# A row LSTM on normalised images: the first row of one half moved into the statistics, late rows moved from GpSimd to ScalarE

## The chip, the cores and the metric

The kernel runs on one core of a Trainium2 chip. The metric is the device time of one execution in microseconds. Five engines work side by side, each through its own list of instructions in order: TensorE (PE in the profile, with PEld for its weight loads), VectorE (DVE), ScalarE (ACT), GpSimd (POOL) and SyncE (SP), which here issues every transfer. An engine waits only where an instruction needs what another engine or a transfer has not delivered yet.

## The reference

The input x has 8 images of 96 channels, 128 rows and 128 columns. It is normalised in 32 groups of 3 channels (mean and variance over channels, rows and columns of a group), run through a row LSTM, and added to the result.

```python
its = conv(X, W_is * mask)                 # 1x3, masked, 96 -> 384 channels
def step(carry, row_in):                   # over the 128 rows
    h, c = carry
    ss = conv1d(h, W_ss)                   # 3 taps along the columns
    g5 = (ss + row_in).reshape(B, 3, 4, Oc, Wd)
    f, i, o = sigmoid(g5[:, :, 0]), sigmoid(g5[:, :, 1]), sigmoid(g5[:, :, 2])
    g = tanh(g5[:, :, 3])
    c_new = f * c + i * g
    h_new = o * tanh(c_new)
x = x + row_lstm(gn(x))
```

A row cannot start before the row above has its h, so the 128 rows are a chain. Nothing can be normalised before an image's statistics are known, so x is read twice: once for the statistics, once, in blocks of rows, for the recurrence.

## The kernel before

**Statistics.** An image is read as 128 partitions of 12288 numbers, in 6 chunks of 2048 columns (1 MB each; 48 chunks in all), into a ring of 6 buffers, so that chunk k of every image uses buffer k. VectorE runs `bn_stats` (L669) on 4 pieces of 512 columns per chunk and `bn_aggr` (L675) per image. Chunk 2 of the first seven images goes to ScalarE instead: `sums_of` (L198) has GpSimd write the negative of one column (`base`, L199), and ScalarE sums differences and squares (L200, L203). `merge` (L205) joins both shares on GpSimd, `Scale` (L225) makes scale and shift of a half's four images with small matmuls (L237) and 8-column operations. SyncE issues the next chunk into a buffer as soon as its reader is done; `chunks` (L641) puts other loads into that order, by the number of chunks issued.

**The recurrence.** The images are split into two halves of four. A half-step is one row of one half; half-step n is row n//2 of half n%2, so the two halves alternate, and half-step n needs h of n-2. Each half-step has 21 matmuls (in the trace two records each): own products of the input (P, Q, E: L376 from `xs`), and four products of h with the three-tap weights, written with sums and differences of even and odd columns (`vs`, `vf` by VectorE, `vd` by GpSimd, L476). ScalarE or VectorE copies the first partial result (`m`, L416/L418), VectorE adds and subtracts (L421, L425), ScalarE makes the gates (L428, L432), VectorE the cell and h (L436 to L453). The order is written out by hand in `PERIOD` and `PRODUCTS`, by short names, and no scheduler changes it on TensorE, ScalarE, VectorE and GpSimd.

**Rows in blocks of 4.** Channels 64 to 95 of the input are normalised into `hx` beside h (`normalise_shared`, L331, "shared"). Channels 0 to 63 stand twice in `xr`; `own_image` (L318) widens one image's four rows (normalise into `xw`, L297), and `combine` (L308) writes even+odd and two differences into `xs`. Both run on GpSimd during the block before: `work(n)` (L527) says which parts follow half-step n in `finish(n)` (L545), after its `vd` and residual; `FIRST` (L516) lists them for the first eight half-steps. `load_rows` loads `xr`, `load` loads x itself.

**The seam.** `events` (L628) places work of half 0 among the statistics, by image and piece: its merge and scales in image 4, its rows in images 4 to 6, and half-step 0 inside image 7 up to its gates. After the last aggregation come half 1's scales (on VectorE), its first row (`own_row`, L324, widened on ScalarE), the rest of half-step 0, and half-step 1. Rows 1 to 3 of half 1's first block, the late rows, are loaded then (L691, L692) and normalised by GpSimd in `late(1)` to `late(3)` after half-steps 0, 1 and 3, one image and row at a time.

Of the kernel before, what the change touches and what calls it, by code (L numbers as in the profile page):

```python
# [7 lines left out]
F32 = mybir.dt.float32  # L8
AF = mybir.ActivationFunctionType
ALU = mybir.AluOpType  # L10
# [5 lines left out]
def strided(ap, offset, dims):  # L16

    return bass.AP(ap.tensor, ap.offset + offset, [ap.ap[0], *[list(d) for d in dims]])
# [3 lines left out]
def kernel(  # L22
# [3 lines left out]
    w: bass.AP,  # L26


    out: bass.AP,
):  # L30

# [22 lines left out]
    nc = tc.nc  # L54
    B, C, H, W = x.shape
    P = 128
    NH = 2
    BH = B // NH
# [16 lines left out]

    O4 = 4 * C
    wl = const.tile([P, w.shape[1]], F32, name="wl")
    wm = const.tile([P, 3, O4], F32, name="wm")
    wx = const.tile([P, 2, O4], F32, name="wx")
    tap = [wl[:, bass.ts(i, O4)] for i in range(5)]  # L80
    bias, bias2 = wl[:, 5 * O4 : 5 * O4 + 3], wl[:, 5 * O4 + 3 : 5 * O4 + 6]
    gm = wl[:, 5 * O4 + 6 :].rearrange("p (i q) -> p i q", i=3)
    wt = [tap[1], wm[:, 0, :], wm[:, 1, :], tap[2]]
    wo = [wx[:, 0, :], wx[:, 1, :], tap[3]]

    def load_weights():
        nc.sync.dma_start(wl, w)

    def make_weights():

# [82 lines left out]
                skip_group_check=True,  # L173
            )

    def first_rows(s, hi):

        t = xt[s, 0].rearrange("c b r w -> c b (r w)")[:, :, 0 : hi * W]
        nc.scalar.activation(t[C:P], t[C2:C], AF.Identity)
        for p in range(2):  # L180
            nc.scalar.activation(  # L181
                xr[s][p * C2 : (p + 1) * C2, :, 0 : hi * W], t[0:C2], AF.Identity
            )

# [4 lines left out]

    SHARE = CH / QW
    su = const.tile([P, B, 2], F32, name="su")
    base = const.tile([P, B], F32, name="base")

    def sums_of(b, xc):  # L198
        nc.gpsimd.tensor_scalar(base[:, b : b + 1], xc[:, 0:1], -1.0, None, ALU.mult)  # L199
        nc.scalar.activation(  # L200
            xc, xc, AF.Identity, bias=base[:, b : b + 1], accum_out=su[:, b, 0:1]
        )
        nc.scalar.activation(xc, xc, AF.Square, accum_out=su[:, b, 1:2])  # L203

    def merge(s, n):  # L205

        p = nc.gpsimd
        at = slice(s * BH, s * BH + n)
        u, v, t = su[:, at, 0], su[:, at, 1], const.tile([P, n], F32, name=f"mt{s}")
        mean, var = st[s][:, 0:n, 0], st[s][:, 0:n, 1]  # L210
        p.tensor_scalar(su[:, at, :], su[:, at, :], 1.0 / CH, None, ALU.mult)
        p.tensor_mul(t, u, u)
        p.tensor_sub(v, v, t)
        p.tensor_sub(u, u, base[:, at])
        p.tensor_sub(u, u, mean)
        p.tensor_scalar(t, u, SHARE, None, ALU.mult)
        p.tensor_add(mean, mean, t)
        p.tensor_mul(u, u, u)
        p.tensor_scalar(u, u, SHARE * (1.0 - SHARE), None, ALU.mult)
        p.tensor_sub(v, v, var)  # L220
        p.tensor_scalar(v, v, SHARE, None, ALU.mult)
        p.tensor_add(var, var, v)
        p.tensor_add(var, var, u)
# [70 lines left out]
        else:  # L294
            engine.tensor_scalar(dst, src, scale, shift, ALU.mult, ALU.add)  # L295

    def widen(engine, xw, i, n, s, j, lo):  # L297

        norm(
            engine,  # L300
            strided(xw[:, i, :], 0, [(W + 1, n), (J + 1, 2), (1, J)]),
            xr[s][:, j, lo * W : (lo + n) * W].rearrange("p (r j t) -> p r t j", r=n, t=2),
            0,
            1,
            s * BH + j,
        )
# [14 lines left out]
        widen(nc.gpsimd, xw[0], 0, R, s, j, 0)  # L321
        combine(xw[0], R, to[:, :, 0, j, :], to[:, :, 1:3, j, :])

    def own_row(engine, xw, s, r):  # L324

        to = xs[s][0]
        for j in range(BH):
            widen(engine, xw, j, 1, s, j, r)
        combine(xw, BH, to[:, r, 0], to[:, r, 1:3].rearrange("p t b j -> p b t j"))

    def normalise_shared(engine, s, k, j, lo, hi):  # L331
# [21 lines left out]
    class HalfStep:  # L353
# [31 lines left out]
        def own(self, a, i):  # L385

            low = a == order["A"] or (a == order["C"] and self.s == 0)
            rhs = self.xs[:, i].rearrange("p b j -> p (b j)")
            self.mm(a, i % 2, wo[i], rhs, slice(0, C2) if low else slice(C2, P))
# [111 lines left out]
        )  # L501

    SHARED = ((0,), (1,), (2, 3), ())

    def own(s, *images):
        return [(own_image, s, 1, j) for j in images]

    def shared(s, k, *images, rows=(0, R)):  # L510
        return [(normalise_shared, nc.gpsimd, s, k, j, *rows) for j in images]

    def late(r):
        return shared(1, 0, *range(BH), rows=(r, r + 1)) + [(own_row, nc.gpsimd, xw[0], 1, r)]

    FIRST = [  # L516
        late(1) + own(0, 0),
        late(2) + shared(0, 1, 0),
        own(0, 1, 2),
        late(3) + [(load_rows, 1, 1)] + shared(0, 1, 1),  # L520
        own(0, 3) + [(load_rows, 0, 2)] + shared(0, 1, 2, 3) + own(1, 0),
        own(1, 1, 2) + shared(1, 1, 0, 1),
        own(1, 3) + [(load_rows, 1, 2)] + shared(1, 1, 2, 3),
        [(own_image, 0, 2, 0)],
    ]

    def work(n):  # L527
        if n < len(FIRST):
            return FIRST[n]
        row, s = divmod(n, NH)  # L530
        k, r = divmod(row, R)
        parts = []
        if r == R - 1 and k + 2 < NB:
            parts.append((own_image, s, k + 2, 0))
        elif r < R - 1 and k + 1 < NB:
            parts.append((own_image, s, k + 1, r + 1))
        if k + 1 < NB:
            parts += shared(s, k + 1, *SHARED[r])
        if r == R - 2 and k + 2 < NB:
            parts.append((load_rows, s, k + 2))  # L540
        if n == len(FIRST):
            parts.append((own_image, 1, 2, 0))
        return parts

    def finish(n):  # L545
# [66 lines left out]
    NS = QW // SN  # L612
    A = Scale(0)

    def shared_rows(engine, s, hi):
        for j in range(BH):
            normalise_shared(engine, s, 0, j, 0, hi)

    def begin():
        do(-NH, "S F D")  # L620
# [3 lines left out]
    def at(image, n):  # L624
        return image * NS + n


    events = {  # L628
        at(4, 0) + 2: lambda: (merge(0, BH), A.means()),
        at(4, 0) + 8: lambda: (A.squares(nc.scalar), A.to_sbuf(), first_rows(0, R)),  # L630
        at(4, 0) + 16: lambda: (A.scale(nc.gpsimd), shared_rows(nc.scalar, 0, R)),
        at(5, 12): lambda: (own_image(0, 0, 0), own_image(0, 0, 1)),
        at(6, 12): lambda: (own_image(0, 0, 2), own_image(0, 0, 3)),
        at(6, 18): lambda: first_rows(1, 1),
        at(7, 1): lambda: (merge(1, BH - 1), spin(10, stats[6])),
        at(7, 6): begin,
        at(7, 11): lambda: do(0, "loA hiA"),
        at(7, 13): lambda: do(0, "loB hiB EA 0A 3A taA siA"),
        at(7, 15): lambda: do(0, "loC hiC EB EC 0B 3B taB siB 0C 3C"),
    }  # L640
    chunks = {  # L641
        6: load_weights,
        7: make_weights,
        16: lambda: load(0, 0, copy=False),
        40: lambda: load(1, 0, 0, 1, copy=False),
    }
    stats = []
# [1 line left out]
    for b in range(B):  # L649
        bst = g_pool.tile([P, NS, 6], F32, tag="bst", name=f"bst{b}")  # L650
        xb = x[b].rearrange("c h w -> (c h w)").rearrange("(p q) -> p q", p=P)
        done = 0
        for k in range(QW // CH):
            xc = ring[n % len(ring)]
            pieces = 2 if n in (0, B * QW // CH - 1) else 1
            for piece in range(pieces):
                size = CH // pieces
                nc.sync.dma_start(  # L658
                    xc[:, bass.ts(piece, size)], xb[:, bass.ds(k * CH + piece * size, size)]
                )  # L660
            n += 1
            if n in chunks:
                chunks[n]()
            by_act = k == 2 and b + 1 < B
            if by_act:
                sums_of(b, xc)
            for j in range(CH // SN):
                if not by_act:
                    nc.vector.bn_stats(bst[:, done, :], xc[:, bass.ts(j, SN)])  # L669
                    done += 1  # L670
                m += 1
                if m in events:
                    events[m]()
        stats.append(bst[:, 0:done, :].rearrange("c n s -> c (n s)"))
        nc.vector.bn_aggr(st[b // BH][:, b % BH, :], stats[b])  # L675

    do(0, "taC siC")
    Bh = Scale(1)
    Bh.means()
    do(0, "fg")  # L680
    Bh.squares(nc.vector)
    spin(5, wt[0][:, 0:256])
    do(0, "gt")
    Bh.scale(nc.vector)

    shared_rows(nc.vector, 1, 1)
    do(1 - NH, "S F")
    own_row(nc.scalar, xw[1], 1, 0)
    do(1 - NH, "D")
    do(0, "ce th")  # L690
    load_rows(1, 0, 1, R)  # L691
    load(1, 0, 1, R)  # L692
    for s in range(NH):
        if s == 0:
            load_rows(0, 1)
        load(s, 1)


    do(1, "1A 2A 1B 2B 1C 2C PA PB QA QB P+A PC QC cpA loA hiA cpB loB hiB cpC loC hiC")
    do(1, "ou' F' S' D' re'")  # L700
    for n in range(1, last + 2):
        for names in PERIOD:
            do(n, PRODUCTS[n % 2] if names == "X" else names)
# [53 lines left out]
```

## Time and profile before

Seven runs: median 2087.94 us, 2087.39 to 2088.57.

| what | value |
|---|---|
| the profiled execution's own time | 2087.81 us |
| its span, first to last instruction | 2086.0 us |
| busy: TensorE, VectorE, GpSimd, ScalarE | 93%, 82%, 69%, 63% |
| last `bn_aggr` ends | 138.89 us |
| first matmul of half-step 1 starts | 146.37 us |
| TensorE busy from 160 to 220 us | 18.18, 18.00 and 16.47 of each 20 us |
| TensorE busy from 220 us on | 20.00 of 20 us |

TensorE is busy all the time from about 220 us to the end. Before that the span falls into the statistics, where the transfers run at 370 to 430 GB/s, and a stretch of some 80 us in which the recurrence has begun but TensorE still has gaps. In the lines of a timeline the columns are the start, the time, the engine, the line of the kernel, the operation, output<-input, the shapes, the count, and in brackets how long the engine had idled before and what ended that.

### The profile page before, as it was taken

The page shows a single profiled execution, that of the slowest core. Times are in us where ns is not written, and L with a number is a line of the kernel's source. Part 1 is how long each engine was busy: PE and PEld are TensorE (multiplying, and loading weights), DVE is VectorE, ACT ScalarE, POOL GpSimd, SP SyncE. Part 2 cuts the span into 40 slices and gives each one's busy share as a digit, 9 for nine tenths or more (in the row PEclk, how much of TensorE's full clock was granted, in tenths as well). Part 3 has the DMA queues.
Part 4 walks back from the last instruction along what each step waited for, and adds up shares of the span by engine and source line. Part 5 has one row for each costly group of instructions (what it writes and reads, how often), then busy time and mean ns, then how long its engine had stood idle before and what let it go on. Part 6 is the DMA issues. An engine that isn't in the chain of part 4 may idle for free.

```text
span 2086.0 us, 31236 instructions
## 1 busy us (share of the span) xinstructions
PE 1949.4 (93%) x10810; PEld 1586.1 (76%) x10810; DVE 1703.5 (82%) x3522; ACT 1321.2 (63%) x2352; POOL 1445.8 (69%) x1636
## 2 busy tenths in 40 slices
PE   0069999999999999999999999999999999999998
PEld 0047788888888888888888888888888888888886
DVE  6877788888888888888888888888888888888887
ACT  2435666666666666666666666666666666666666
POOL 2229877777777777777777777777777777777762
PEclk9989999999999999999999999999999999999999
DMA  9982344433333444333344433333444333344411
GB/s 389 407 289 54 91 111 112 111 94 77 89 89 98 112 111 112 80 79 85 91 112 112 112 96 76 89 89 98 112 111 112 81 78 85 91 112 112 112 31 31
DMA packets 103243, 236.43 MB, mean 113 GB/s; under 512 B 5936, under 2 KB 8880, under 8 KB 97072
## 3 DMA queue, kind: packets, MB, share of 16 engines
q1 hardware_dynamic: 103088, 234.45, 40.7%
q8 instruction: 87, 1.43, 0.3%
q14 instruction: 68, 0.56, 0.1%
HBM read 184.09 MB, written 50.33 MB: 112 GB/s over the span
## 4 chain that ended last, share of the span: by engine, by line
PE 91%; DMA 3%; DVE 2%; POOL 2%; ACT 1%; issue 0%; SPq 0%; POOLq 0%
PE ps L376 91%; DVE bst L669 2%; DMA piece<-in_x_dram 2%; DMA wl<-in_w_dram 1%; DMA xs<-in_x_dram 1%; POOL hx L295 0%; POOL xw L295 0%; PE spin L167 0%; ACT piece L200 0%; POOL vd L476 0%; POOL xs L312 0%; SPq L658 0%; ACT piece L203 0%; POOL x L493 0%; ACT xr L181 0%
## 5 line engine op out<-in xcount | busy, mean ns | idle before, releaser
L376 PE MATMUL ps<-vd,wl 128*128 128x256 f32 x3072 | 816.9, 388 | 5.0 <-POOL vd L476 4.2
L428 ACT ACTIVATE g<-ps 32x512 f32<-32x512 f32 x768 | 453.6, 591 | 468.0 <-PE ps L376 459.7
L376 PEld LDWEIGHTS ps<-vd,wl 128*128 128x128 f32 x3072 | 562.7, 190 | 158.3 <-issue 86.2
L476 POOL TENSOR_TENSOR vd<-hx 128x512 f32<-128x512 f32 x256 | 266.0, 1039 | 467.9 <-DVE vs L466 464.9
L376 PE MATMUL ps<-xs,wx 64*128 64x256 f32 x3072 | 457.5, 394 | 3.1 <-POOL xs L311 2.5
L376 PE MATMUL ps<-vs,wm 128*128 128x256 f32 x1536 | 457.5, 379 | 0.0
L376 PE MATMUL ps<-vf,wm 128*128 128x256 f32 x1536 | 457.1, 379 | 0.0
L432 ACT ACTIVATE ps<-ps 96x512 f32<-96x512 f32 x768 | 418.9, 572 | 16.5 <-PE ps L376 0.2
L376 PEld LDWEIGHTS ps<-xs,wx 64*128 64x128 f32 x3072 | 322.7, 187 | 112.1 <-issue 84.2
L436 DVE TENSOR_TENSOR ps<-ps,c 96x512 f32<-96x512 f32 x256 | 177.9, 695 | 268.1 <-ACT ps L432 268.1
L425 DVE TENSOR_TENSOR ps<-m,ps 128x256 f32<-128x256 f32 x768 | 329.3, 429 | 26.4
L421 DVE TENSOR_TENSOR ps<-m,ps 128x256 f32<-128x256 f32 x768 | 324.9, 423 | 8.8
L493 POOL TENSOR_TENSOR x<-x,hx 96x512 f32<-96x512 f32 x254 | 328.7, 1294 | 0.0
L376 PEld LDWEIGHTS ps<-vs,wm 128*128 128x128 f32 x1536 | 291.9, 190 | 40.4 <-issue 0.5
L376 PEld LDWEIGHTS ps<-vf,wm 128*128 128x128 f32 x1536 | 292.1, 190 | 39.9
L418 ACT ACTIVATE m<-ps,wl 128x256 f32<-128x256 f32 x513 | 243.2, 474 | 88.9 <-PE ps L376 75.3
L312 POOL TENSOR_TENSOR xs<-xw 128x512 f32<-128x512 f32 x256 | 273.6, 1069 | 0.0
L376 PE MATMUL ps<-xs,wl 64*128 64x256 f32 x1536 | 264.7, 376 | 1.5 <-DVE ps L425 1.3
L446 ACT ACTIVATE th<-c 96x512 f32<-96x512 f32 x256 | 161.2, 630 | 106.7 <-DVE c L442 106.7
L295 POOL TENSOR_SCALAR hx<-x,rstd,nmr 32x512 f32<-32x512 f32 (+1 forms) x260 | 206.0, 792 | 26.7
L376 PEld LDWEIGHTS ps<-xs,wl 64*128 64x128 f32 x1536 | 195.1, 187 | 20.2 <-DVE ps L425 3.0
L295 POOL TENSOR_SCALAR xw<-xr,rstd,nmr 128x512 f32<-128x512 f32 (+1 forms) x264 | 209.0, 792 | 1.0
(84 smaller groups left out, 1243.7 us busy)
## 6 DMA issues: line engine op xcount, KB each, us to landing
xr<-in_x_dram SPq DMA_DIRECT2D x124, 512.0 KB, 6.4
x<-in_x_dram SPq DMA_DIRECT2D x63, 768.0 KB, 5.8
out_dram<-x SPq DMA_DIRECT2D x62, 768.0 KB, 4.6
xs<-in_x_dram SPq DMA_DIRECT2D x30, 1024.0 KB, 12.8
piece<-in_x_dram SPq DMA_DIRECT2D x16, 1024.0 KB, 11.3
x<-in_x_dram SPq DMA_DIRECT2D x62, 256.0 KB, 3.1
xs<-in_x_dram SPq DMA_DIRECT2D x4, 512.0 KB, 8.6
wl<-in_w_dram SPq DMA_DIRECT2D x1, 1155.0 KB, 16.8
```

Of the source, the lines that this page charges most:

```text
L295: engine.tensor_scalar(dst, src, scale, shift, ALU.mult, ALU.add)
L312: nc.gpsimd.tensor_sub(differences, strided(xw[:, 0, :], 0, [(W + 1, n), (J, 2), (1, J)]), strided(xw[:, 0, :], J + 1, [(W + 1, n), (0, 2) ...
L376: nc.tensor.matmul(self.ps[a][:, bass.ts(half, HB)], weights[rows, bass.ts(a, P)], rhs[rows], start=new, stop=False, skip_group_check=True,)
L418: nc.scalar.activation(self.m1[a], m1, AF.Identity, bias=column)
L421: nc.vector.tensor_add(self.ps[a][:, 0:HB], self.m1[a], self.ps[a][:, HB:])
L425: nc.vector.tensor_sub(hi, self.m1[a], hi)
L428: nc.scalar.activation(self.g[a * 32 : (a + 1) * 32], self.ps[a][C:P], AF.Tanh)
L432: nc.scalar.activation(gate, gate, AF.Sigmoid)
L436: nc.vector.tensor_mul(f, f, self.c)
L446: nc.scalar.activation(self.th, self.c, AF.Tanh)
L476: diff = nc.gpsimd.tensor_sub(self.vd.rearrange("p t (b j) -> p t b j", b=BH), strided(h, 1, [(BH * JP - 1, 2), (JP, BH), (1, J)]), stride ...
L493: (nc.gpsimd if row + 1 < NT else nc.vector).tensor_add(xo, xo, self.h)
```

## The change

- **Half-step 0 wholly within the statistics.** Half 0's merge moves one piece earlier and its scales up to ten pieces; its rows are copied by ScalarE already during image 3 (three `first_rows` calls, one copy each); its own images, its matmuls and gates move from images 5 to 7 into images 4 and 5; forget, cell, output, residual and the sums for its next row are placed in image 6, where before they stood behind the last aggregation.
- **ScalarE sums chunks 2 and 4 of seven images** instead of chunk 2 alone (`BY_ACT`); `base` is still one column, of chunk 2. `merge` adds the two shares first.
- **The late rows**: their loads (L691, L692 before) now stand right behind the statistics, ahead of half 1's scales. ScalarE widens rows 1 to 3 of each image in one instruction into `late`, a view of a ring buffer, whose middle columns GpSimd clears first; GpSimd combines them row by row; ScalarE also normalises the shared channels of these rows. All of this stands ahead of half-step 1.
- **GpSimd's first blocks**: `FIRST` no longer has late rows; it spreads block 1 over half-steps 0 to 6 anew; both halves' first image of block 2 follow half-step 7. `load_rows(1, 1)` stands ahead of the recurrence.
- **Weights**: the two own taps are loaded once, on 64 partitions, into `wt2`, and ScalarE copies them to the other 64.
- The load of half 0's first block is issued two chunks earlier; the matmuls that only keep TensorE running (`spin`) move from piece 1 to piece 20 of image 7's order.

```diff
@@ load_weights
         nc.sync.dma_start(wl, w)
+        nc.sync.dma_start(wt2[0:C2].rearrange("p t c -> p (t c)"), w_own)
+        nc.scalar.activation(wt2[C2:P], wt2[0:C2], AF.Identity)
...
-    def first_rows(s, hi):
+    def first_rows(s, hi, homes=(0, 1, 2)):
...
-    SHARE = CH / QW
+    BY_ACT = (2, 4)
+    SHARE = len(BY_ACT) * CH / QW
...
+        p.tensor_add(su[:, 0, at, :], su[:, 0, at, :], su[:, 1, at, :])
...
-    def own_row(engine, xw, s, r):
+    def own_row(xw, s, r):
         to = xs[s][0]
-        for j in range(BH):
-            widen(engine, xw, j, 1, s, j, r)
         combine(xw, BH, to[:, r, 0], to[:, r, 1:3].rearrange("p t b j -> p b t j"))
...
-    FIRST = [
-        late(1) + own(0, 0),
-        late(2) + shared(0, 1, 0),
-        own(0, 1, 2),
-        late(3) + [(load_rows, 1, 1)] + shared(0, 1, 1),
-        own(0, 3) + [(load_rows, 0, 2)] + shared(0, 1, 2, 3) + own(1, 0),
-        own(1, 1, 2) + shared(1, 1, 0, 1),
-        own(1, 3) + [(load_rows, 1, 2)] + shared(1, 1, 2, 3),
-        [(own_image, 0, 2, 0)],
-    ]
+    FIRST = [own(0, j) + shared(0, 1, j) for j in range(BH)] + [
+        [(load_rows, 0, 2)] + own(1, 0) + shared(1, 1, 0, 1),
+        own(1, 1, 2),
+        own(1, 3) + [(load_rows, 1, 2)] + shared(1, 1, 2, 3),
+        [(own_image, 0, 2, 0), (own_image, 1, 2, 0)],
+    ]
...
-        at(4, 0) + 2: lambda: (merge(0, BH), A.means()),
-        at(4, 0) + 8: lambda: (A.squares(nc.scalar), A.to_sbuf(), first_rows(0, R)),
-        at(4, 0) + 16: lambda: (A.scale(nc.gpsimd), shared_rows(nc.scalar, 0, R)),
-        at(5, 12): lambda: (own_image(0, 0, 0), own_image(0, 0, 1)),
-        at(6, 12): lambda: (own_image(0, 0, 2), own_image(0, 0, 3)),
-        at(6, 18): lambda: first_rows(1, 1),
-        at(7, 1): lambda: (merge(1, BH - 1), spin(10, stats[6])),
-        at(7, 6): begin,
-        at(7, 11): lambda: do(0, "loA hiA"),
-        at(7, 13): lambda: do(0, "loB hiB EA 0A 3A taA siA"),
-        at(7, 15): lambda: do(0, "loC hiC EB EC 0B 3B taB siB 0C 3C"),
+        at(3, 1): lambda: first_rows(0, R, (0,)),
+        at(3, 13): lambda: first_rows(0, R, (1,)),
+        at(3, 21): lambda: first_rows(0, R, (2,)),
+        at(4, 1): lambda: (merge(0, BH), A.means()),
+        at(4, 4): lambda: (A.squares(nc.scalar), A.to_sbuf()),
+        at(4, 6): lambda: A.scale(nc.gpsimd),
+        at(4, 14): lambda: (own_image(0, 0, 0), own_image(0, 0, 1)),
+        at(4, 20): lambda: shared_rows(nc.scalar, 0, 0, R),
+        at(5, 2): lambda: (own_image(0, 0, 2), own_image(0, 0, 3)),
+        at(5, 13): begin,
+        at(5, 17): lambda: do(0, "loA hiA"),
+        at(5, 19): lambda: do(0, "loB hiB EA 0A 3A taA siA"),
+        at(5, 21): lambda: do(0, "loC hiC EB EC 0B 3B taB siB 0C 3C taC siC"),
+        at(6, 7): lambda: do(0, "fg"),
+        at(6, 9): lambda: do(0, "gt"),
+        at(6, 12): lambda: do(0, "ce th"),
+        at(6, 18): lambda: do(0, "ou F S D re"),
+        at(6, 22): lambda: first_rows(1, 1),
+        at(7, 1): lambda: merge(1, BH - 1),
+        at(7, 20): lambda: spin(10, stats[6]),
...
-        16: lambda: load(0, 0, copy=False),
+        14: lambda: load(0, 0, copy=False),
...
-            by_act = k == 2 and b + 1 < B
+            by_act = k in BY_ACT and b + 1 < B
...
-    do(0, "taC siC")
+    load_rows(1, 0, 1, R)
+    load(1, 0, 1, R)
     Bh = Scale(1)
     Bh.means()
-    do(0, "fg")
     Bh.squares(nc.vector)
     spin(5, wt[0][:, 0:256])
-    do(0, "gt")
     Bh.scale(nc.vector)
-    shared_rows(nc.vector, 1, 1)
+    shared_rows(nc.vector, 1, 0, 1)
     do(1 - NH, "S F")
-    own_row(nc.scalar, xw[1], 1, 0)
+    for j in range(BH):
+        widen(nc.scalar, xw[1], j, 1, 1, j, 0)
+    own_row(xw[1], 1, 0)
     do(1 - NH, "D")
-    do(0, "ce th")
-    load_rows(1, 0, 1, R)
-    load(1, 0, 1, R)
+    late = ring[2][:, 0 : (R - 1) * BH * (W + 1)].rearrange("p (r q) -> p r q", q=W + 1)
+    nc.gpsimd.memset(late[:, :, J : J + 1], 0.0)
+    for j in range(BH):
+        widen(nc.scalar, late, j, R - 1, 1, j, 1, step=BH)
+    for r in range(1, R):
+        own_row(late[:, (r - 1) * BH : r * BH], 1, r)
+    shared_rows(nc.scalar, 1, 1, R)
+    load_rows(0, 1)
     for s in range(NH):
-        if s == 0:
-            load_rows(0, 1)
         load(s, 1)
+    load_rows(1, 1)
...
-    do(1, "ou' F' S' D' re'")
```

## The prediction

> **What bounds the kernel now.** I write half-step n for row n//2 of half n%2, and h(n) for the end of VectorE's L453, which makes its h. I read the page first, then VectorE's timeline at L453, then what TensorE waits for between 140 and 230 us, then every engine's timeline around the start of the recurrence.
>
> ```profile
> span 2086.0 us, 31236 instructions
> PE 1949.4 (93%) x10810; PEld 1586.1 (76%) x10810; DVE 1703.5 (82%) x3522; ACT 1321.2 (63%) x2352; POOL 1445.8 (69%) x1636
> ...
> PE 91%; DMA 3%; DVE 2%; POOL 2%; ACT 1%; issue 0%; SPq 0%; POOLq 0%
> ```
>
> TensorE carries 91% of the chain that ended last; what is left to win lies before its steady run. The timeline at L453 shows where that starts:
>
> ```profile
> 153.78 0.68 DVE L453 TENSOR_TENSOR hx<-ps,th 96x512 f32<-96x512 f32 x1
> ...
> 161.97 0.68 DVE L453 TENSOR_TENSOR hx<-ps,th 96x512 f32<-96x512 f32 x1
> ...
> 225.62 0.68 DVE L453 TENSOR_TENSOR hx<-ps,th 96x512 f32<-96x512 f32 x1
> ...
> 233.00 0.68 DVE L453 TENSOR_TENSOR hx<-ps,th 96x512 f32<-96x512 f32 x1
> ...
> 240.66 0.68 DVE L453 TENSOR_TENSOR hx<-ps,th 96x512 f32<-96x512 f32 x1
> ```
>
> These are h(0), h(1), h(8), h(9), h(10). From h(8) on the steps alternate 7.39 and 7.65 us (233.00 and 240.66) and the pair repeats in 15.04. From h(1) to h(8) that would be 4 x 7.65 + 3 x 7.39 = 52.8 us; it took 63.65. So 10.9 us are lost in the first eight half-steps. The waits of TensorE from 140 to 230 us (total, times, longest) name who loses them:
>
> ```profile
> PE ps L376 <- POOL vd L476: 4.2, 3, 2.1
> PE ps L376 <- POOL xs L311: 2.5, 2, 1.3
> PE ps L376 <- DVE ps L425: 0.7, 1, 0.7
> PE ps L376 <- POOL xs L312: 0.6, 2, 0.3
> ```
>
> GpSimd: 7.3 us. Some of the rest is clock, in TensorE's timeline:
>
> ```profile
> 194.48 1.99 PE L376 MATMUL ps<-vd,wl 128*128 128x256 f32 x6 [2.00 <-POOL vd L476]
> 196.40 2.77 PE L376 MATMUL ps<-xs,wx 64*128 64x256 f32 x12
> ...
> 213.86 1.56 PE L376 MATMUL ps<-vd,wl 128*128 128x256 f32 x6 [2.07 <-POOL vd L476]
> ```
>
> After the first wait 12 matmul records take 2.77 us instead of the 1.57 of other stretches; after the second, as long, the clock held. Last, the start of the recurrence:
>
> ```profile
> 120.11 4.23 PE L167 MATMUL spin<-bst,wl 128*128 128x120 f32 x20 [41.60 <-DVE bst L669]
> ...
> 138.09 0.80 DVE L675 BATCH_NORM_AGGREGATE st<-bst 128x2 f32<-128x144 f32 x1
> ...
> 143.97 1.67 ACT L293 ACTIVATE xw<-xr,nmr,rstd 128x128 f32<-128x128 f32 x4 [6.14 <-DVE nmr L284]
> ...
> 147.61 1.03 POOL L476 TENSOR_TENSOR vd<-hx 128x512 f32<-128x512 f32 x1
> ...
> 150.91 0.47 ACT L418 ACTIVATE m<-ps,wl 128x256 f32<-128x256 f32 x1 [2.93 <-PE ps L376]
> ...
> 152.43 1.53 PE L376 MATMUL ps<-vd,wl 128*128 128x256 f32 x6 [0.72 <-DVE ps L425]
> ```
>
> The last aggregation ends at T = 138.9. Everything after hangs on T: scales at T+5, TensorE's first matmul of half-step 1 at T+7.5, GpSimd's vd to T+9.75, ScalarE's first m copy at T+12.
>
> **The change, part by part.** Terms are against this execution (span 2086.0, run 2087.81; the median, 2087.94, is 0.13 above it).
>
> *1. GpSimd's first blocks: -10.9.* Before, GpSimd normalises rows 1 to 3 of half 1 itself in late(1..3): 12 shared pieces at about 0.53 us and 12 widenings at 0.44 to 0.57, some 12 us, of its 64.8 busy us in 155 to 226. These leave. An own image costs 0.80 + 0.64 + 1.06 with gaps = 2.7, a shared piece 0.9, vd 1.04, residual 1.3. So the new lists cost: n = 0 to 3: 5.9 each; n = 4: 6.8; n = 5: 7.7; n = 6: 6.8; n = 7: 7.7, against 7.39 or 7.65 per half-step. The two at 7.7 lag 0.3 and the next has room; in the trace vd came 0.95 us after h in the steady run and 3.8 us after h(1) and h(2) with TensorE waiting only 0.2. Half 1's image 0 of block 2, moved from list 8 to 7, waits for its rows: their load goes out after image 3's widening and lands 9.6 us later (215.85 to 225.4 in the transfers before), and the queue ahead needs about 9.5: 0 to 0.3, within that slack. The three rows' combinings, 1.7 each, stay on GpSimd before list 0, end at T+18, and half-step 3 needs row 1 not before T+22. The loads moved ahead on SP (rows 1 to 3 of half 1, block 1 of both halves) go behind the last statistics piece in the queue: 4.7 MB, which at the 235 GB/s of the four transfers after that piece (1.9 MB in 8.1 us) take 20 us and have landed by T+16; the first is read from T+18, apart from rows 1 to 3 (rival D). I take all 10.9; bounds: 7.3 (the waits alone) and 10.9.
>
> *2. A new wait: ScalarE between half-step 1 and its copies: +2.45.* ScalarE now does four widenings of 128x384 and four shared pieces of 32x384 before the two m copies of half-step 1. The first writes the buffer whose middle column GpSimd clears only behind vd (its order), so ScalarE starts at T+10.05, although free since T+6.8. One costs between 0.42 (128x128, 1.67 / 4) and 0.865 (32x512, 3.46 / 4 at 88.75); by length 0.72. Eight: 5.7, so free at T+15.8, copy to T+16.3, VectorE's sum to T+16.75, and TensorE's third weight product of that step, in order and with all later work behind it, runs at T+16.85 instead of T+14.4. Ends: 0.42 each gives 0.1, 0.865 gives 3.6.
>
> *3. Clock after that stall: +0.8.* 2.45 us is the length of the two waits shown; one was followed by a slow stretch that cost some 1.7 us, one was not. Half of 1.7; ends 0 and 1.7. [...]
>
> *4. The end of the statistics: -1.2.* VectorE gives up one chunk of 4 x 0.62 us in seven images, but the last image, 24 x 0.62 = 14.9, is unchanged, and in the trace VectorE finished it 5 us behind its data (last piece landed 133.65): 3 us of half-step 0 stood inside it. Those move to images 5 and 6. What ends last there is ScalarE. Its chunk of image 4 waits for GpSimd's subtrahend, behind the whole scale chain: merging can start at 72.8 (image 3 aggregated); 14 small operations of GpSimd 3.6, TensorE and ScalarE 2.8 (75.75 to 78.55 before), VectorE's two with the waits 0.9, GpSimd's scale 3.9 (82.81 to 86.74) and the subtrahend 0.3: 84.4. Then two chunks at 4.15, four shared pieces 3.46, the next image's chunk: 100.6. Half-step 0's own products follow the own images (GpSimd, 84.4 + 4 x 2.66 = 95.1) on a TensorE idle for 15 us: the spin at 120.11 took 4.23 for 20 records of 120 columns, as long per record (0.21) as 256 columns take when warm, so it began slow. 12 records at 0.43 then 4 of A: first copy at 101 to 102, and VectorE's sums from 101 to 102.4. From there VectorE has no gap: tails 5.7, image 6 with the rest of half-step 0 14.2, image 7 14.9, aggregation 0.8: T = 136.6 to 138.0. (ScalarE stays just ahead: from 103.8 a chunk 4.15, a table load and six gates 4.8, a chunk 4.15, the cell's tanh 0.6 make 117.5, where VectorE wants it at 117.6.) I take 137.7. Floor: data, 133.65 + 1.24 + 0.8 = 135.7; above, a copy later by 1.5 gives 139.5. So -3.2 to +0.6.
>
> *5. At nothing.* The split weights: 0.2 MB less to load, one 64x768 copy on ScalarE (0.8) that holds GpSimd's weight making by as much, before chunk 2 of image 1, whose buffer was reissued at 37.15 with transfers queued to 40.9. Three first_rows copies of 1.91 lie in image 3, where ScalarE has 13.9 us of work in 14.9; without that cover they would go into term 4. Block 0's early load goes two chunks sooner, same bytes. The spin waits on image 6's statistics, done near 122: it no longer warms anything, but before, too, the clock stood at 0.5 from 135 to 145.
>
> Sum: -10.9 + 2.45 + 0.8 - 1.2 = -8.85: 2087.94 - 8.85 = 2079.1.
>
> **Rivals.**
> *A. More is won:* ScalarE's eight cost 0.5 each, no slow clock, T at 136.6: -10.9 + 0.8 - 2.3 = -12.4, 2075.5. For it: one stall kept its clock. Against: the cold start.
> *B. ScalarE bounds the statistics:* two chunks (8.3 us) plus extras in 14.9 us per image; if each lateness reaches the refill of its buffer, transfers starve as at 88.79, where a late chunk cost 1.2. Twice more, and T at 141: +2.1 instead of -1.2, 2082.4.
> *C. GpSimd still bounds the first block:* lists 5 and 7 stall as list 4 and 6 do now (two waits of 2 us with one slow clock): 5 to 6 of the 10.9 stay: 2084.6.
> *D. Slower:* the first row's reads on VectorE (second image on) and ScalarE are made to wait for the load of rows 1 to 3, whose address range spans theirs. Scales are ready at T+5, 143. It decides when the load lands past 152, 18 us after the last piece; the four transfers after that piece took 8.1 in the trace. At 157, 5 us beyond: 2093. This load already stood late once (issued 145.66, landed 152.93), but behind a wait that it no longer has.
>
> **How the numbers follow.** Forecast 0.62 (own range 2076.5 to 2082), A 0.12, B 0.12, C 0.08, D 0.06. Range 2075.5 (A) to 2084 (just short of C). About 0.2%, 4.2 us, is what a measurement of this kernel can tell from no change: faster below 2083.8 holds the forecast, A, most of B and a quarter of C, 0.84; C's rest and half-way D 0.11; slower 0.05.
>
> **What would show it.** h(1) near 163, with h(1) to h(8) at 52.8 and no wait on POOL vd over 1 us (term 1); a wait of some 2.4 us on VectorE's sum near T+14.4, ScalarE's m copy near T+15.8 (2); records of 0.43 us or not behind it (3); the last aggregation near 137.7 without a half-step's operations in image 7 (4). Wrong if T passes 141, if own images still wait for loads, or if VectorE's shared pieces after the scales wait on a DMA.

## The result, and the profile after

The changed kernel takes 2081.97 us (median of 13 runs, 2080.96 to 2083.43), the kernel before 2088.27 us in the runs beside it (33 runs, 2086.61 to 2090.66). The ratio is 0.997, with a 95% interval of 0.9963 to 0.9977: faster, by 6.3 us. The forecast was 2079.1 us, with a range of 2075.5 to 2084.0.

The profiled execution has a span of 2080.4 us and took 2082.19 us, 0.22 above the median. The head of its page, with the shares of the chain that ended last:

```profile
span 2080.4 us, 31230 instructions
PE 1951.8 (94%) x10810; PEld 1588.3 (76%) x10810; DVE 1685.2 (81%) x3494; ACT 1355.6 (65%) x2389; POOL 1433.5 (69%) x1615
...
PE 92%; ACT 2%; DMA 2%; DVE 2%; POOL 1%; issue 0%; SPq 0%; ACTq 0%; POOLq 0%; DVEq 0%
```

TensorE did the same 10810 records and bounds the kernel as before. Where the start of its steady run now lies is read from the timeline of VectorE's output multiply, which is line 461 now (columns as before: start, time, engine, line, operation):

```profile
117.52 0.69 DVE L461 TENSOR_TENSOR hx<-ps,th 96x512 f32<-96x512 f32 x1 [1.35 <-ACT th L454]
...
166.23 0.68 DVE L461 TENSOR_TENSOR hx<-ps,th 96x512 f32<-96x512 f32 x1
...
219.28 0.68 DVE L461 TENSOR_TENSOR hx<-ps,th 96x512 f32<-96x512 f32 x1
...
227.34 0.68 DVE L461 TENSOR_TENSOR hx<-ps,th 96x512 f32<-96x512 f32 x1
```

These are h(0), h(1), h(8) and h(9). h(0) lies inside the statistics now. From h(1) to h(8) it takes 53.05 us where it took 63.64, but h(1) comes at 166.91, later than the 162.65 of before. The waits of TensorE between 138 and 230 us (total, times, longest) have lost GpSimd and gained a long one on VectorE:

```profile
PE ps L384 <- DVE ps L433: 4.1, 2, 3.3
PE ps L384 <- DVE vs L474: 0.5, 1, 0.5
```

The timelines of the engines between the last aggregation and half-step 1's third weight product show whose wait it is:

```profile
136.22 0.81 DVE L682 BATCH_NORM_AGGREGATE st<-bst 128x2 f32<-128x144 f32 x1
...
146.86 0.12 POOL L699 MEMSET piece<- 128x12 f32 x1
147.02 3.04 ACT L302 ACTIVATE piece<-xr,nmr,rstd 128x384 f32<-128x384 f32 x4 [3.11 <-POOL piece L699]
150.08 3.01 ACT L302 ACTIVATE hx<-x,nmr,rstd 32x384 f32<-32x384 f32 x4
153.11 0.84 ACT L426 ACTIVATE m<-ps,wl 128x256 f32<-128x256 f32 x2
...
153.62 0.43 DVE L429 TENSOR_TENSOR ps<-m,ps 128x256 f32<-128x256 f32 x1 [3.63 <-ACT m L426]
154.08 0.43 DVE L433 TENSOR_TENSOR ps<-m,ps 128x256 f32<-128x256 f32 x1
...
154.57 1.22 PE L384 MATMUL ps<-vd,wl 128*128 128x256 f32 x2 [3.33 <-DVE ps L433]
155.72 2.50 PE L384 MATMUL ps<-xs,wx 64*128 64x256 f32 x9
```

VectorE's end of the statistics is T = 137.03. ScalarE then idles 3.11 us for a clearing of 0.12 us on GpSimd, does its eight late operations in 6.05 us, and only then the copies that VectorE's sums and TensorE need. And the two records behind the wait take 1.22 us, the next nine 2.50 (0.70 and 1.34 at full clock, in e3 below): TensorE has cooled, that is, its granted clock has been halved. That clock (third column from the end, before the DMA share and the GB/s), in slices of 2 us from 154 on (from 144 to 154 it was 1.00):

```profile
154.00:156.00 2.00, 1.43 (x4) 0.78 (x6) 1.24 (x4) 0.00 (x0) 1.92 (x4) 0.53 1.06 131
156.00:158.00 2.00, 2.00 (x10) 1.58 (x11) 0.00 (x0) 0.00 (x0) 1.89 (x3) 0.50 1.04 165
158.00:160.00 2.00, 2.00 (x9) 1.18 (x6) 0.00 (x0) 0.47 (x1) 0.48 (x1) 0.50 0.88 187
160.00:162.00 2.00, 2.00 (x9) 1.67 (x8) 0.93 (x2) 1.82 (x4) 0.00 (x0) 0.76 0.11 34
```

A slice of 2 us at mean clock c was at half speed for 4 x (1 - c) us: 1.88 + 2.00 + 2.00 + 0.96 = 6.84 us here. The two spans differ by 5.65 us, and the stretches add up to it:

| stretch | before | after | difference | predicted |
|---|---|---|---|---|
| T, end of the last aggregation | 138.90 | 137.03 | -1.87 | -1.2 |
| T to the third weight product of half-step 1 | 14.39 | 17.54 | +3.15 | +2.45 |
| that product to h(1) | 9.36 | 12.34 | +2.98 | +0.8 |
| h(1) to h(8) | 63.64 | 53.05 | -10.59 | -10.9 |
| h(8) to h(9) | 7.39 | 8.06 | +0.67 | 0 |
| sum | | | -5.66 | -8.85 |

### The profile page after: what moved, and what is told of

Read it like the earlier page. It is cut to its first block, busy times and chain, and to the rows that moved or that the text cites. A ratio compares the mean times of both kernels' runs of the same rounds, so it can differ in the third digit from the quotient of the medians.

```text
span 2080.4 us, 31230 instructions
## 1 busy us (share of the span) xinstructions
PE 1951.8 (94%) x10810; PEld 1588.3 (76%) x10810; DVE 1685.2 (81%) x3494; ACT 1355.6 (65%) x2389; POOL 1433.5 (69%) x1615
## 4 chain that ended last, share of the span: by engine, by line
PE 92%; ACT 2%; DMA 2%; DVE 2%; POOL 1%; issue 0%; SPq 0%; ACTq 0%; POOLq 0%; DVEq 0%
PE ps L384 92%; DMA piece<-in_x_dram 1%; DMA wt<-in_w_own_dram 1%; DVE bst L676 1%; ACT piece L208 0%; ACT piece L211 0%; ACT g L436 0%; ACT xs L208 0%; ACT xs L211 0%; PE pv L246 0%; POOL xs L322 0%; POOL xs L321 0%; POOL xw L304 0%; SPq L665 0%; ACT piece L302 0%
## 5 line engine op out<-in xcount | busy, mean ns | idle before, releaser
L433 DVE TENSOR_TENSOR ps<-m,ps 128x256 f32<-128x256 f32 x768 | 329.3, 429 | 26.4
L384 PE MATMUL ps<-xs,wt 64*128 64x256 f32 x1536 | 264.9, 377 | 0.1
L304 POOL TENSOR_SCALAR hx<-x,rstd,nmr 32x512 f32<-32x512 f32 x248 | 200.1, 807 | 25.5
L384 PEld LDWEIGHTS ps<-xs,wt 64*128 64x128 f32 x1536 | 195.3, 188 | 18.5 <-DVE ps L433 0.9
L304 POOL TENSOR_SCALAR xw<-xr,rstd,nmr 128x512 f32<-128x512 f32 x252 | 202.7, 804 | 0.7 <-DMA xr<-in_x_dram 0.2
```

Source lines behind the costliest of these rows:

```text
L384: nc.tensor.matmul(self.ps[a][:, bass.ts(half, HB)], weights[rows, bass.ts(a, P)], rhs[rows], start=new, stop=False, skip_group_check=True,)
L433: nc.vector.tensor_sub(hi, self.m1[a], hi)
```

## The experiments

The ratios of these eleven kernels are to the kernel before in the same set of runs (2088.2 to 2088.7 us). T and h(1) come from each one's profile.

| kernel | median us (range) | ratio, 95% interval | T | T to h(1) | h(1) to h(8) |
|---|---|---|---|---|---|
| e1_clear_early | 2075.69 (2075.14 to 2076.97) | 0.9939, 0.9926 to 0.9953 | 137.47 | 23.74 | 53.0 |
| e2_shared_behind | 2075.99 (2075.28 to 2077.05) | 0.9941, 0.9928 to 0.9953 | 138.57 | 23.46 | 53.0 |
| e3_fill_gap | 2079.58 (2079.37 to 2079.98) | 0.9958, 0.9944 to 0.9971 | 138.01 | 26.93 | 53.0 |
| e11_idle_29 | 2080.32 (2079.26 to 2081.80) | 0.9957, 0.9943 to 0.9970 | 137.48 | 28.46 | 53.1 |
| e12_idle_20 | 2079.27 (2078.96 to 2081.39) | 0.9953, 0.9940 to 0.9967 | 139.97 | 26.94 | 53.0 |
| e6_late_on_gpsimd | 2084.11 (2082.81 to 2086.07) | 0.9978, 0.9969 to 0.9987 | 139.43 | 23.31 | 60.6 |
| e4_no_late_rows | 2081.35 (2079.60 to 2081.69) | 0.9965, 0.9951 to 0.9978 | 140.41 | 23.17 | 56.6 |
| e5_one_chunk | 2077.14 (2075.77 to 2077.21) | 0.9945, 0.9931 to 0.9958 | 138.77 | 23.91 | 53.0 |
| e7_base_early | 2075.29 (2074.41 to 2076.33) | 0.9937, 0.9925 to 0.9950 | 137.11 | 23.74 | 53.0 |
| e9_warm_seam | 2075.53 (2074.44 to 2077.98) | 0.9943, 0.9929 to 0.9957 | 137.19 | 22.83 | 53.0 |
| e10_together | 2076.24 (2073.99 to 2077.91) | 0.9937, 0.9924 to 0.9951 | 137.15 | 23.93 | 53.0 |

**Take the wait away: the clearing earlier.** GpSimd clears the middle columns of `late` before half 1's first row instead of behind its `vd`:

```diff
     Bh.scale(nc.vector)
+    late = ring[2][...]
+    nc.gpsimd.memset(late[:, :, J : J + 1], 0.0)
     shared_rows(nc.vector, 1, 0, 1)
...
     do(1 - NH, "D")
-    late = ring[2][...]
-    nc.gpsimd.memset(late[:, :, J : J + 1], 0.0)
```

> The changed kernel with one instruction moved: GpSimd clears the middle columns of the late buffer before half 1's first row instead of behind vd, so ScalarE can begin the late widenings as soon as the row-0 widenings are done (T+6.9 instead of T+10.0). Theory (the 6.1 us lost between the last aggregation T and h(1) are 3.1 us of waiting for ScalarE's m copy and 3.0 us of half clock that this idle stretch of TensorE brings): m copy at T+13 instead of T+16.1, third product near T+15, no slow stretch, h(1) at T+24.3 to T+25 instead of T+29.9, time 2076.5 to 2077.5. Rival (the slow stretch comes from TensorE having stood idle since half-step 0 was moved into the statistics, whatever ScalarE does): the wait goes but the 3 us of half clock stay, h(1) near T+27.5, 2079.5.

Measured: 2075.69 us, 6.3 less than the changed kernel, and the ranges don't touch. Its timelines at the same place:

```profile
128.71 0.12 POOL L693 MEMSET piece<- 128x12 f32 x1 [4.09 <-DVE bst L676]
...
144.25 3.04 ACT L302 ACTIVATE piece<-xr,nmr,rstd 128x384 f32<-128x384 f32 x4
147.31 3.03 ACT L302 ACTIVATE hx<-x,nmr,rstd 32x384 f32<-32x384 f32 x4
150.37 0.84 ACT L426 ACTIVATE m<-ps,wl 128x256 f32<-128x256 f32 x2
...
150.76 1.76 PE L384 MATMUL ps<-vd,wl 128*128 128x256 f32 x6 [0.72 <-DVE ps L433]
```

The eight late operations take as long as ever, but start at T+6.78 and end as TensorE delivers. All six records of the three weight products run in one group, with the 0.72 us of wait that the kernel before had too; T to h(1) is back at 23.74 (before: 23.75). The time is even 0.8 us under the theory's range, and the rival's slow clock did not come. One clearing of 0.12 us in the wrong place in GpSimd's order had cost both the wait and the clock.

**Half the operations behind the copies.** To see whether the late work on ScalarE still costs anything once it may start on time, its four shared pieces go behind the copies as well:

```diff
 # on top of the earlier clearing
-    shared_rows(nc.scalar, 1, 1, R)
...
     do(1, "1A 2A 1B 2B 1C 2C ... cpA loA hiA cpB loB hiB cpC loC hiC")
+    shared_rows(nc.scalar, 1, 1, R)
```

> As the run with the early clearing, and ScalarE's four shared pieces of the late rows stand behind half-step 1's m copies. Theory: ScalarE is free at T+10, the copies wait for nothing but TensorE (T+11.9 as in the kernel before), third product at T+14.2, h(1) at T+23.5 to T+24, time 2075.5 to 2076.5; about 0.7 us faster than with the early clearing alone. Rival (clock from the long idle time before): 2079.

Measured: 2075.99 us, which the runs can't tell from 2075.69. T to h(1) is 0.28 shorter in the profile, and T itself 1.1 later; the 0.7 us that the theory gave this move did not come. So at T+6.8 ScalarE's eight operations were hidden already, to within 0.3 us.

**Keep the wait, take the clock away.** The gap stays, but seven spinning matmuls fill it, put ahead of the third weight product (`0B`) in TensorE's order; `do` passes over what is done already:

```diff
         for names in PERIOD:
+            if n == 1 and names.startswith("3A"):
+                do(n, "3A")
+                spin(7, wt[0][:, 0:256])
             do(n, PRODUCTS[n % 2] if names == "X" else names)
```

> The changed kernel with seven matmuls into an unread bank put on TensorE into the gap before half-step 1's third weight product (some 3.0 us at full clock); ScalarE's order is unchanged, so the wait stays. It tells wait and clock apart. Theory: third product still near T+17.5, but no slow stretch behind it, h(1) near T+27, 3 us earlier, 2079. Rival (the slow stretch has another cause than this gap): the slow stretch stays, 2082.

Measured: 2079.58 us, 2.4 less than the changed kernel. TensorE's timeline:

```profile
152.04 3.19 PE L171 MATMUL spin<-wl 128*128 128x256 f32 x14
155.55 0.70 PE L384 MATMUL ps<-vd,wl 128*128 128x256 f32 x2 [0.32 <-DVE ps L433]
156.18 1.34 PE L384 MATMUL ps<-xs,wx 64*128 64x256 f32 x9
```

The product starts at T+17.54, exactly as in the changed kernel, but its records run at 0.22 us instead of 0.43. T to h(1) falls by 2.95 us (29.88 to 26.93), and none of it from the wait. This is the price of the clock; what is left over e1, 26.93 - 23.74 = 3.19, is that of the wait.

**How much idle time cools TensorE?** The same with one and with three spinning matmuls, so that some 2.7 and 2.1 us stay idle:

```diff
-                spin(7, wt[0][:, 0:256])
+                spin(1, wt[0][:, 0:256])     # e12: spin(3, ...)
```

> The changed kernel with one spinning matmul (two records of 0.22 us) instead of seven at the start of the gap ahead of half-step 1's third weight product: some 2.9 us of the 3.33 stay idle. Without the slow clock the time was 2079.6, with it 2082.0. Theory (an idle time of 2 to 3 us cools TensorE in some executions and not in others, as the waits of 2.00 and 2.07 us of the kernel before did): the runs lie in two groups or near 2081 to 2082, and the profile shows matmul records of 0.43 us behind the gap or not. Rival (only the whole 3.3 us cool it): all runs within 0.4 us of 2079.6.

> The same with three spinning matmuls: some 2.0 us stay idle, the length of the waits that did both before. Theory: some runs near 2079.6, some up to 2 us above; fewer slow ones than with 2.9 us idle. Rival (only the whole 3.3 us cool it): all runs within 0.4 us of 2079.6.

TensorE in the first, and its clock in the slices of 2 us:

```profile
155.00 0.70 PE L384 MATMUL ps<-vd,wl 128*128 128x256 f32 x2 [2.68 <-DVE ps L433]
155.62 2.19 PE L384 MATMUL ps<-xs,wx 64*128 64x256 f32 x9
```

```profile
154.00:156.00 2.00, 1.00 (x6) 0.65 (x8) 1.62 (x4) 0.38 (x2) 2.00 (x3) 0.99 1.11 207
156.00:158.00 2.00, 2.00 (x12) 1.64 (x10) 0.00 (x0) 0.00 (x0) 1.92 (x3) 0.50 1.03 156
158.00:160.00 2.00, 2.00 (x10) 1.23 (x7) 0.00 (x0) 0.84 (x2) 0.81 (x2) 0.65 0.96 205
```

And in the second:

```profile
157.53 0.70 PE L384 MATMUL ps<-vd,wl 128*128 128x256 f32 x2 [2.07 <-DVE ps L433]
158.16 1.34 PE L384 MATMUL ps<-xs,wx 64*128 64x256 f32 x9
```

After 2.68 us of idling the clock stays full for another microsecond, then is halved for 0.04 + 2.00 + 1.40 = 3.44 us: T to h(1) is 28.46, 1.53 above the filled gap. After 2.07 us it holds (1.00 in every slice from 148 to 164 us), and T to h(1) is 26.94. So it can take less than the whole 3.3 us to cool the array, and e11's rival falls; whether the 2.07 us of e12 ever cool it, its one profile doesn't decide. How often either length does it, the times don't tell: e11's four runs lie between 2079.26 and 2081.80, and the slowest of e12 (2081.39) is the profiled one, in which T, not the clock, is late by 2 us.

**Only GpSimd's lists as before.** The changed kernel with the late rows back on GpSimd and `FIRST` as it was; half-step 0 stays inside the statistics, and ScalarE's second chunk too:

```diff
-    FIRST = [own(0, j) + shared(0, 1, j) for j in range(BH)] + [...]
+    FIRST = [
+        late(1) + own(0, 0),
+        late(2) + shared(0, 1, 0),
+        ...                            # as before the change
+    ]
...
-    for j in range(BH):
-        widen(nc.scalar, late, j, R - 1, 1, j, 1, step=BH)
-    ...
-    shared_rows(nc.scalar, 1, 1, R)
```

> The changed kernel with the late rows and the lists of the first eight half-steps put back as in the kernel before (rows 1 to 3 of half 1 on GpSimd, one image and row at a time); statistics and half-step 0 stay changed. Theory: T and the first matmul as in the changed kernel, h(1) at T+23.8, h(1) to h(8) 63.6 us again, so 6.1 us won and 10.6 lost: 2086.4. Rival (the stalls of the first block came from late half-step-0 work and the late loads, not from the late rows): h(1) to h(8) under 57, 2079.

Measured: 2084.11 us, between the two. TensorE's waits:

```profile
PE ps L384 <- POOL vd L484: 3.8, 3, 2.1
...
PE ps L384 <- POOL xs L321: 0.4, 1, 0.4
```

h(1) to h(8) takes 60.6 instead of 63.6. GpSimd's timeline says why: with half-step 0 done early, the first list (late row 1 and an own image) runs from 149.42 to 157.80, before h(1), where the kernel before ran it from 157.83 to 166.50 and held back `vd` of half-step 1 behind it. So 3 us of what the prediction gave to the lists can be had from half-step 0's place alone.

**Only the late rows away.** The kernel before, without them (their slots hold zeros):

```diff
     def late(r):
-        return shared(1, 0, *range(BH), rows=(r, r + 1)) + [(own_row, nc.gpsimd, xw[0], 1, r)]
+        return []
```

> The kernel before, without its late rows: rows 1 to 3 of half 1's first block are not normalised, their slots hold zeros, so GpSimd has some 22 us less to do behind half-steps 0, 1 and 3 (three times four shared pieces, four widenings and two combinings). Everything else is as before: half-step 0 behind the last aggregation, one chunk on ScalarE, the loads where they were. Theory (the late rows on GpSimd are the whole price of the first eight half-steps): h(1) to h(8) falls from 63.6 to about 53 us, h(1) stays at T+23.7, time 2088.3 - 10.6 = 2077.7. Rival (the other lists, or the loads behind them, hold TensorE once the late rows are gone): h(1) to h(8) stays above 57, time above 2081.5.

Measured: 2081.35 us, at the border of the rival. (The late rows are less work than the 22 us expected: twelve shared pieces at 0.53, twelve widenings at 0.44 and six combinings at 0.64 or 1.06 make some 17.) TensorE still waits for GpSimd, all of it between 205 and 212 us:

```profile
PE ps L379 <- POOL vd L479: 1.6, 1, 1.6
PE ps L379 <- POOL xs L314: 1.2, 1, 1.2
```

The late rows are 7.1 of the 10.8 us that h(1) to h(8) could lose (63.64 to 56.58); the other 3.8 lie in the old lists 4 to 6 themselves, which put 5 own images and 6 shared pieces behind three half-steps. Both halves of the term, the late rows and the re-spreading, were needed.

**ScalarE's second chunk given back to VectorE**, on e1:

```diff
-    BY_ACT = (2, 4)
+    BY_ACT = (2,)
```

> The changed kernel with the clearing moved ahead (e1_clear_early, 2075.7), but ScalarE sums chunk 2 alone of seven images, as before the change; VectorE takes chunk 4 back, 4 x 0.62 us per image. Theory (the second chunk on ScalarE makes the room in images 5 and 6 in which half-step 0 fits): T about 2.5 us later, 2078.2. Rival (the statistics end with the data, or with the chain through ScalarE, whatever VectorE has to do): within 0.6 us of 2075.7.

Measured: 2077.14 us, 1.45 above e1 in the median, with T 1.3 later: between the theory (2.5) and the rival (0.6). The ranges of the two overlap (2075.77 to 2077.21, 2075.14 to 2076.97), and profiles of kernels with the same statistics differ in T by more than that, so the size is rough. VectorE's waits between 97 and 137 us shrink from 3.7 us in e1 to 0.8 in e5: a part of the 2.5 us that the chunk costs VectorE goes into time in which it had waited for ScalarE and data anyway.

**ScalarE's chain in image 4 begun earlier**, on e1: the scale chain behind the subtrahend.

```diff
-        at(4, 6): lambda: A.scale(nc.gpsimd),
+        at(4, 9): lambda: A.scale(nc.gpsimd),
```

> e1_clear_early with one move: GpSimd's scale chain of half 0 stands three pieces later, so behind the subtrahend of image 4's chunk instead of ahead of it; ScalarE's sums of image 4 should start near 79.7 us instead of 84.7. Theory (beyond that chain it is the last data and the cold products of half-step 0 that set the end of the statistics): ScalarE's chunk starts 4 to 5 us earlier, and the time falls by no more than 0.8: 2074.9 to 2075.7. Rival (this chain of ScalarE alone sets T, as the prediction's fourth term has it): T earlier by 1.5 to 2 us, 2073.9.

Measured: 2075.29 us, inside the theory, and 0.4 below e1, which the runs can't tell from nothing. ScalarE's timeline:

```profile
80.40 2.00 ACT L208 ACTIVATE piece<-piece,base 128x2048 f32<-128x2048 f32 x1
...
96.03 2.00 ACT L208 ACTIVATE piece<-piece,base 128x2048 f32<-128x2048 f32 x1 [3.99 <-POOL base L207]
...
100.82 0.47 ACT L426 ACTIVATE m<-ps,wl 128x256 f32<-128x256 f32 x1 [0.66 <-PE ps L384]
```

The chunk starts at 80.40 instead of the 84.93 of e1, and the 4.5 us are lost again at 96.03: the next subtrahend stands behind four own images on GpSimd. The first copy then waits for TensorE's products, two records of which take 1.06 us there and 0.59 us three microseconds later. T moves by 0.36.

**TensorE kept warm up to T**, on e1, and the three moves together:

```diff
-        at(7, 20): lambda: spin(10, stats[6]),
+        at(7, 17): lambda: spin(15, bst[:, 0:16, :].rearrange("c n s -> c (n s)")),
```

> e1_clear_early with the spinning matmuls of image 7 moved from a point near 121 us to one near 132: fifteen instead of ten, on that image's own statistics of its first sixteen pieces, so that TensorE is at full clock when the last aggregation ends. Theory (the clock at half speed from 135 to 145 us costs the scale chain of half 1 its two cold steps): the small group matmuls take half of their 0.56 and 0.99 us, scales 0.7 us sooner, 2074.7 to 2075.1. Rival (those matmuls are bound by something other than the clock, or the gap after the spin cools TensorE again): 2075.7, or later by the spin's overhang.

> The changed kernel with three moves together: the clearing ahead of half 1's first row (e1_clear_early, 2075.7), the scale chain behind the subtrahend of image 4 (e7_base_early, 0.4 better) and the spin near 132 us (e9_warm_seam, 0.9 shorter from T to h(1) in its profile). Theory (they act at different places, and the end of the last load bounds T): T 137.0, h(1) at T+22.9, 2074.5. Rival (the moves inside the statistics shift which of VectorE and the data comes last and add nothing): 2075.6.

Measured: 2075.53 and 2076.24 us, neither told from e1. In both, the group matmuls behind T take 0.59 us where e1's took 0.99, so the spin does warm TensorE: its clock was 1.00 from 138 to 140 us in both, and 0.50 in e1. What happens next is in their TensorE timelines, first e9's, then e10's:

```profile
143.65 0.67 PE L384 MATMUL ps<-vs,wm 128*128 128x256 f32 x2 [2.20 <-DVE vs L474]
```

```profile
143.78 1.19 PE L384 MATMUL ps<-vs,wm 128*128 128x256 f32 x2 [2.21 <-DVE vs L474]
```

TensorE idles 2.2 us for VectorE's first sums in both, and cools in e10 (3.40 us at half clock) and not in e9 (1.00 from 138 to 152 us): T to h(1) is 22.83 and 23.93. None of these beats e1 or e7 beyond the spread; the fastest version that the runs support is the changed kernel with the clearing moved (0.9939).

## Why the prediction was right, and where it was off

The time fell within the range and on the forecast's side; it lies at the upper end of the likeliest case's own range (2076.5 to 2082), 2.9 us above the value. The profile's own terms are off by 3.2 us in sum, and terms 2 and 3 carry 2.9 of it. Terms 4 and 5 miss by 0.67 each in opposite directions and cancel; that, and so the place just inside 2082, is luck.

- **Term 1, GpSimd's first blocks: -10.9, measured -10.59.** Right in size; h(1) to h(8) came to 53.05 where 52.8 was forecast, without a wait on `vd`. Its working was too simple: it put all of it on the late rows and the new lists. The runs split it into 7.1 for the late rows and 3.8 for the old lists 4 to 6 (e4), and show that 3 us could also be had by half-step 0's earlier end alone (e6); these overlap.
- **Term 2, the new wait: +2.45, measured +3.15.** Right in place and cause. ScalarE started at T+9.99 (forecast T+10.05), its operations took 0.76 us (0.72), and the copies came at T+16.1 to T+16.9. What was missing is one step at the end: the third product waits for VectorE's second sum (L433, 0.43 us) too, not for the first alone. The price by difference of two kernels, e3 against e1, is 3.19.
- **Term 3, the clock: +0.8, measured +2.98.** This is the term that was mis-sized: it came from one slow stretch of the trace (1.7 us, halved for doubt), with 1.7 as its upper end, for a stall of 2.45 us. TensorE idled 3.33 us, and the slow stretch was 6.84 us long, twice the 3.40 us of the kernel before. e3 took 2.95 us of it away without touching the wait. What makes a stretch 6.84 us long here and 3.40 or 3.44 us in four other profiles, no run shows.
- **Term 4, the end of the statistics: -1.2, measured -1.87 in the one profile.** The chain was met step by step: the subtrahend's chunk began at 84.75 (84.4 forecast), the first copy at 100.44 (101 to 102), and behind the sum that waited until 102.46 VectorE had one wait, of 1.35 us. But no single profile gives this term: seven kernels with the same statistics have T from 137.03 to 139.97, mean 138.3, and the two with the old statistics 138.90 and 140.41. By these means it is -1.4. That ScalarE's chain alone sets it isn't so: 4.5 us less there were worth no more than 0.4 (e7), since GpSimd's own images and the data are as late; nor, it seems, does VectorE alone, since 2.5 us more there cost about 1.45 (e5).
- **Term 5, at nothing.** Rival D did not come: half 1's first row never waited for the load of rows 1 to 3. The loads behind it landed later than the first term had it, the last at 161.88 us, T+24.9, instead of by T+16, and nothing waited for them. The image moved to list 7 was given "0 to 0.3 within slack" and cost 0.67 in this profile, for a reason that the term didn't have. Its wait for data was only 0.24 us, but its two combinings on GpSimd ran exactly beside VectorE's sums of h(8), in the timeline of VectorE and GpSimd:

```profile
219.07 0.81 POOL L304 TENSOR_SCALAR xw<-xr,rstd,nmr 128x512 f32<-128x512 f32 x1 [0.24 <-DMA xr<-in_x_dram]
219.96 0.64 POOL L321 TENSOR_TENSOR xs<-xw 128x256 f32<-128x256 f32 x1
219.99 0.89 DVE L479 TENSOR_TENSOR vf<-hx 128x256 f32<-128x256 f32 x1
220.56 1.25 POOL L322 TENSOR_TENSOR xs<-xw 128x512 f32<-128x512 f32 x1
220.81 1.28 DVE L474 TENSOR_TENSOR vs<-hx 128x256 f32<-128x256 f32 x1
```

The sums, 0.42 us elsewhere, took 0.89 and 1.28, and TensorE waited 0.49 for the second. In e3 the same image waited 1.84 us for its data and cost nothing, as the combinings came behind the sums: h(8) to h(9) was 7.39.

Of the rivals, A's time (2075.5) is what e1 reaches, by another way: not because the eight operations are cheaper, but because they may start 3 us sooner. B and C did not happen: T was not past 141, and no wait on GpSimd was left.

## What to carry to other kernels

When a piece of work is moved to another engine, look for the smallest instruction that it waits for and where that one stands in its own engine's order: here 0.12 us of clearing behind a 1 us operation cost 6.3 us, as much as the whole change won. What a wait of TensorE costs in clock should be priced by separate cases, as the traces at hand have them, and not by a mean between them: here waits of 2.0 to 2.7 us were followed by no half clock or by some 3.4 us of it, and one of 3.33 us by 6.84 us; filling the wait with matmuls that nobody reads took that price away here (e3) without a change of order. And a term that is smaller than the spread of its point between profiles needs medians or several profiles, not one.

## What the runs showed of the hardware

**The stretches at half clock behind waits of the recurrence lasted 3.40 to 3.44 us, or 6.84 us.** Worked out from the slices of 2 us as above, for TensorE's waits of 1.6 us or more behind half 1's scales:

| kernel, TensorE resumes at | waited, us | half clock, us |
|---|---|---|
| changed kernel, 154.57 | 3.33 | 6.84 |
| e11, 155.00 | 2.68 | 3.44 |
| e10, 143.78 | 2.21 | 3.40 |
| e9, 143.65 | 2.20 | 0 |
| before, 213.86 | 2.07 | 0 |
| e12, 157.53 | 2.07 | 0 |
| e6, 210.82 | 2.06 | 3.40 |
| before, 194.48 | 2.00 | 3.40 |
| e4, 207.72 | 1.61 | 0 |

The slices of the kernel before, behind its wait at 194.48:

```profile
194.00:196.00 2.00, 1.52 (x6) 1.17 (x6) 1.86 (x5) 0.44 (x1) 2.00 (x3) 0.87 1.07 220
196.00:198.00 2.00, 2.00 (x10) 1.34 (x10) 0.30 (x1) 0.00 (x0) 1.92 (x3) 0.50 0.40 74
198.00:200.00 2.00, 2.00 (x17) 1.42 (x13) 0.00 (x0) 0.34 (x1) 1.80 (x3) 0.78 0.84 219
```

That is 0.52 + 2.00 + 0.88 = 3.40 us. Three of the six waits between 2.00 and 2.21 us cooled the array and three did not, so the length of the wait alone doesn't tell: 2.00 us were followed by half clock and 2.20 us were not. The clock fell up to a microsecond after TensorE had resumed (195.48 against 194.48 here, 155.96 against 155.00 in e11).

The times between the changes of the clock have a pattern too. These are e10's slices in which its clock changes, and the one between:

```profile
136.00:138.00 2.00, 2.00 (x16) 2.00 (x16) 1.27 (x3) 0.00 (x0) 0.00 (x0) 0.80 1.13 234
142.00:144.00 2.00, 0.22 (x1) 0.25 (x2) 1.86 (x6) 1.97 (x6) 0.60 (x1) 0.91 1.07 202
144.00:146.00 2.00, 2.00 (x5) 1.55 (x6) 0.42 (x1) 1.93 (x3) 2.00 (x3) 0.50 1.05 230
146.00:148.00 2.00, 2.00 (x8) 1.51 (x6) 0.00 (x0) 1.91 (x4) 2.00 (x4) 0.74 1.06 230
```

The clock rises at 136.80, falls at 143.64 and rises at 147.04. Slices of 0.2 us place the changes at 134.03 (falls), 147.68, 195.47 and 198.88 in the kernel before, and at 143.89 (rises), 154.13 and 160.96 in the changed kernel. The times between neighbouring changes are 6.84 and 3.40 us in e10, 13.65, 47.79 and 3.41 in the kernel before, 10.24 and 6.83 in the changed kernel: each lies within 0.05 us of 2, 1, 4, 14, 1, 3 and 2 times 3.41 us. The fall at 134.03, inside the statistics, came after a wait of 1.28 us that ended at 132.77, where e4's wait of 1.61 us was followed by none. What sets the step of 3.41 us, and what decides which waits are followed by half clock, no run shows.

**VectorE's sums took longer in the changed kernel where they began beside a running operation of GpSimd: 0.46 to 1.28 us.** VectorE's sums of 128x256 took 0.42 us alone and 0.89 and 1.28 beside GpSimd's combinings, the longer of which grew as well (1.25 for 1.07). In the rows shown at term 5 each sum ends 0.28 us after the combining that was running when it began (220.88 against 220.60, 222.09 against 221.81). All 35 sums of the changed kernel that begin beside a running operation of GpSimd end 0.27 to 0.29 us after it, 31 of them beside a normalisation with one input; the other 477 sums took 0.41 to 0.43 us. In the kernel before 38 of 45 do; of the other 7, three end 0.30 to 0.37 us after GpSimd's operation and four before it, where that operation took 0.95 to 1.22 us. VectorE's gates' product of 96x512, which reads the partial results (`ps`), took 0.69 us at 171.85 beside a combining of 171.64 to 172.71, as it did elsewhere in the changed kernel (0.67 to 0.69 in all 256). Why the sums took longer and that product did not, no run shows.

**The end of the statistics differs by up to 3 us between profiles.** T lies between 137.03 (the changed kernel) and 139.97 (e12) in kernels with the same statistics. With the same loads in the same order, in kernels that differ only behind the statistics, the last piece landed at 134.7 us in the changed kernel's profile and at 137.3 in e6's, where VectorE waited 1.26 us for it. What makes the transfers vary was not tried.
